# An attention block and a clustering block over four images: places for the first image's stacked keys, and the order of its start

## The chip, the cores and the metric

The kernel runs on one core of one Trainium2 chip. The metric is device time in microseconds (us), the median of three runs. A profile is of one further execution, with its own time. Engines are named as in the profile: PE (matrix products), PEld (loading of their weights, beside PE), ACT (scalar engine), DVE (vector engine), POOL (GpSimd), SP (the queue that issues most DMAs). POOL and ACT issue DMAs too, in the order of their other instructions.

## The reference

Input are four images of 256 channels and 64 x 64 places, in 32-bit floats. The first layer is self-attention over the N = 4096 places of an image, with keys and queries of 32 channels; the second a block of clustering, a two-layer MLP and a pointwise convolution. The change touches the first layer alone, and of it the first image:

```python
xf = x.reshape(B, Cc, N)
q = jnp.einsum('oc,bcn->bno', wq, xf) + bq
k = jnp.einsum('oc,bcn->bon', wk, xf) + bk[None, :, None]
attn = jax.nn.softmax(jnp.einsum('bnd,bdm->bnm', q, k), axis=-1)
v = jnp.einsum('oc,bcn->bon', wv, xf) + bv[None, :, None]
out = jnp.einsum('bcn,bmn->bcm', v, attn).reshape(B, Cc, H, W)
return gamma[0] * out + x
```

The second layer's parts that appear below are wf (a weight that the kernel turns over at the start, with a bias from the table pv_s), wpw (the pointwise weights, from which POOL makes two blocks) and a few tables of constants.

## The kernel before

The 4096 places of an image are cut into eight blocks of 512 (NB). One block of queries against one block of keys is a *unit*; eight units (GRP) make a block of queries, 64 an image. A unit's scores are made in two halves of 128 x 1024 (`half`, `products`, L471); ACT copies each half from PSUM into the unit's slot (`kept`, L484), DVE takes the running maximum `top` from PSUM (L495). The two PSUM tiles for this (pool ps_s) are a ring: a half must wait until the DVE maximum of the half two before it is done. Later, the *weighting* subtracts the maximum (`exps`, L637), takes exponentials on ACT, forms sums of quarter blocks (`factors`, L660 on DVE, L646 on POOL) and multiplies with the values in seven products for eight (`weigh`, L716, tile av). For these products POOL makes four sums and differences of the value blocks of each group of four (`sums`, L646, called by `added`).

Keys and queries are kept as high and low halves, stacked on 128 partitions: of one block of 512 places, 32 channels times four parts. A projection of four blocks (`projected`, L344) gives PSUM tiles from which ACT makes the high half (L361) and DVE the low one (L362). `straight` (L376) stacks one block by four DMAs of 64 KB from these halves into a tile of 128 x 512; `written` (L372) stores the halves in DRAM by four DMAs of 256 KB, from where later units load their stacked blocks by one DMA (`k_unit`, L449; `q_block`, L443). Stacked keys have two places (tag "k"), so keys u + 2 are not loaded before the scores of unit u are done. For the first image, `staged` projects blocks 0 to 3 of k and q into a tile `st`, and `halved` blocks 4 to 7, each into a tile with the tag "t13".

Values are made in pairs of 128 places (`v_pair`, four matmul instructions, eight passes on PE; L426), in one of two PSUM buffers of the pool ps_m, and copied by ACT (L434). 16 pairs make an image; POOL's group g needs pairs 2g and 2g + 1.

Everything is recorded under a manual schedule: each engine does its instructions in the order in which the functions call them. `alone` (L847) is the order of the first image until its weighting begins; later images do this work in the gaps of the image before. In it:

- `roots` (L218 to L294) does square roots for the constants on DVE and ACT, and loads ACT's table;
- three value pairs, `staged`, three more pairs, the sums of groups 0 to 2 on POOL;
- units 0 to 7. After unit 0, k's second projection; after unit 1, q's; after units 2 to 7 one value pair each (6 to 11), and at the odd ones from 3 a group of sums. `k_straight` stacks keys u + 2 at the end of unit u. `written` stores k0, q0, k1, q1 at the ends of units 1 to 4, on POOL's queue. From u = 3, `load_rest` issues a step of the remaining constants on SP: the weights mix, then fvb and wproj, then gbv, pv_s and a table, and last pool_w and wpw_s with POOL's two instructions on wpw (L187, L188). At u = 5 the second block of queries is loaded, at u = 6 `wf` (L282, L285) turns its weights over;
- `fold`, pair 12, the transposes of the maximum (`turned_over`, tile tt, L557), a half of unit 8, pair 13, sums 6, the maximum as a diagonal (`across`, L564 and L566), its spreading over the partitions by PE (`spread`, tile hold, L627), pair 14, `exps(0)`, `factors(0)`, pair 15, the second half of unit 8, sums 7.

The pool `work` has single tiles with the tags "t4", "rden", "acc" and "t", which only the weighting uses: t4 and acc are first written in `factors(0)`, rden and t after the first block of queries.

Of the kernel before, what the change touches and what calls it, by code (L numbers as in the profile page):

```python
# [9 lines left out]
F32R = mybir.dt.float32r  # L10
# [4 lines left out]
P = 128  # L15
# [3 lines left out]
NB = 512  # L19
# [10 lines left out]
RG, GRP = 4, N // NB  # L30
# [30 lines left out]
def attention_then_cluster_block(  # L61
# [17 lines left out]
    nc = tc.nc  # L79
# [3 lines left out]
    big = ctx.enter_context(tc.tile_pool(name="big", bufs=1))  # L83
# [4 lines left out]
    work = ctx.enter_context(tc.tile_pool(name="work", bufs=2))  # L88
# [242 lines left out]
    def attention(b, xs, ys):  # L331
# [5 lines left out]
        qs, ks, slots, mxs, accs, tops, rdens, ts = {}, {}, {}, {}, {}, {}, {}, {}  # L337

        def projected(which, i, ps):

            col = 1 if which == "k" else 0
            for k in range(KC):
                for r in range(RG):
                    nc.tensor.matmul(  # L344
                        ps[r * D : (r + 1) * D],
                        wqk_s[:, k, col],
                        block(xs, k, 4 * i + r),
                        start=(k == 0),
                        stop=(k == KC - 1),
                    )  # L350

        def halves_of(which, hi, lo, ps):

            col = 1 if which == "k" else 0
            if which not in own:
                own[which] = dram.tile([NBLK // RG, P, 4, NB], F32, tag=which, name=f"{which}_{b}")
            bias = bqk_s[:, col : col + 1]  # L360
            nc.scalar.activation(hi, ps, AF.Identity, bias=bias)  # L361
            nc.vector.scalar_tensor_tensor(  # L362
                lo, ps, bias, hi.bitcast(F32), ALU.add, ALU.subtract
            )

        def part_of(which, c, hi, lo):
            return (hi if c in ((0, 2) if which == "k" else (0, 1)) else lo).bitcast(F32)

        def written(which, i, hi, lo, dma=nc.sync):
            rows = own[which][i]  # L370
            for c in range(4):
                dma.dma_start(out=rows[:, c], in_=part_of(which, c, hi, lo))  # L372

        def straight(which, r, dst, hi, lo, other=nc.sync):
            for c in range(4):
                (other if c % 2 else nc.sync).dma_start(  # L376
                    out=dst[c::4].bitcast(F32),
                    in_=part_of(which, c, hi, lo)[r * D : (r + 1) * D],
                )
# [6 lines left out]
        def staged():  # L386

            st = spool.tile([P, 4, NB], F32R, tag="s", name=f"st_{b}")  # L390
            ps = ps_s.tile([P, 2, NB], F32, tag="s", name=f"pr_{b}")
            k0, q0 = (st[:, 0], st[:, 1]), (st[:, 2], st[:, 3])
            for j, w in enumerate("kq"):
                projected(w, 0, ps[:, j])
            halves_of("k", *k0, ps[:, 0])
            k_straight(0, k0)
            qs[0] = work.tile([P, NB], F32R, tag="q", name=f"q_{b}_0")
            halves_of("q", *q0, ps[:, 1])
            straight("q", 0, qs[0], *q0, nc.scalar)
            k_straight(1, k0)  # L400
            return k0, q0

        def k_straight(u, src):
            ks[u] = big.tile([P, NB], F32R, tag="k", bufs=2, name=f"k_{b}_{u}")
            straight("k", u % RG, ks[u], *src)

        def halved(which, i, write=True):

            ps = ps_m.tile([P, NB], F32, tag="m", name=f"{which}p_{b}_{i}")
            two = work.tile([P, 2, NB], F32R, tag="t13", name=f"hl_{which}_{b}_{i}")  # L410
            projected(which, i, ps)
            halves_of(which, two[:, 0], two[:, 1], ps)
            if write:
                written(which, i, two[:, 0], two[:, 1])
            return two[:, 0], two[:, 1]
# [3 lines left out]
        def v_half(i):  # L419
            if i == 0:  # L420
                own["v"] = big.tile([P, N // P, C], F32, tag="v", name=f"v_{b}")
            if i % 2 == 0:
                vps[0] = ps_m.tile([P, 2, C], F32, tag="m", name=f"vp_{b}_{i // 2}")
            o = (i * P) % XT
            for k in range(KC):
                nc.tensor.matmul(  # L426
                    vps[0][:, i % 2, :],
                    xs[i * P // XT][:, k, o : o + P],
                    wv_s[:, k, :],
                    start=(k == 0),  # L430
                    stop=(k == KC - 1),
                )
            if i % 2:
                nc.scalar.copy(own["v"][:, i - 1 : i + 1, :], vps[0])  # L434

        def v_pair(i):
            v_half(2 * i)
            v_half(2 * i + 1)
# [44 lines left out]
        def kept(u, h, sc):  # L483
            nc.scalar.copy(slots[u][:, PAIR[h]].rearrange("p h r n -> p r h n"), tiles(sc))  # L484
# [3 lines left out]
        def highest_of(nb, src):  # L488


            top = tiles(tops[nb])
            if nb not in saved:
                saved[nb] = src
                return
            nc.vector.tensor_tensor(top, src, top if saved[nb] is None else saved[nb], ALU.max)  # L495
            saved[nb] = None
# [6 lines left out]
        def half(u, h, kept_only=False):  # L503

            nb, g = divmod(u, GRP)
            if h == 0:
                begun(u)
            sc = products(u, h)  # L510
            kept(u, h, sc)
            own_copy = slots[u][:, PAIR[h]].rearrange("p h r n -> p r h n")
            if g == 0 and h == 0:
                highest_of(nb, own_copy)
            elif kept_only:
                held.append(lambda: highest_of(nb, own_copy))
            else:
                return lambda: highest_of(nb, tiles(sc))
            return lambda: None
# [40 lines left out]
        def across(nb, tag="w2", tp=None):  # L560
            if tp is None:
                tp = turned_over(nb, ps_m.tile([P, 4, P], F32, tag="m", name=f"tt_{b}_{nb}"))
            mx = small.tile([P, 4], F32, tag="mx", name=f"mx_{b}_{nb}")
            nc.vector.tensor_reduce(mx, tp, AX.X, ALU.max)  # L564
            dg = work.tile([P, 4, P], F32, tag=tag, bufs=1, name=f"dg_{b}_{nb}")
            nc.vector.tensor_tensor(  # L566
                dg,
                ident.unsqueeze(1).to_broadcast([P, 4, P]),
                mx.unsqueeze(2).to_broadcast([P, 4, P]),
                ALU.mult,  # L570
            )
            return dg
# [272 lines left out]
        dgs, t31, t4s = {}, {}, {}  # L845

        def alone():  # L847

            roots()
            for i in range(3):  # L850
                v_pair(i)
            k0, q0 = staged()
            for i in range(3, 6):
                v_pair(i)

            def added(*gs):
                for g in gs:
                    for f in sums(g):
                        f()

            added(0, 1, 2)
            rest = load_rest()
            for u in range(GRP):
                half(u, 0)()
                if u < GRP - 1:
                    half(u, 1)()
                else:

                    sc = products(u, 1)
                    highest_of(0, tiles(sc))  # L870
                    kept(u, 1, sc)
                if u == 0:
                    k1 = halved("k", 1, False)
                elif u == 1:
                    q1 = halved("q", 1, False)
                else:
                    v_pair(u + 4)
                    if u % 2:
                        added((u + 3) // 2)
                if u < 6:  # L880
                    k_straight(u + 2, k0 if u < 2 else k1)
                if 0 < u < 5:
                    written("kqkq"[u - 1], (u - 1) // 2, *(k0, q0, k1, q1)[u - 1], nc.gpsimd)
                if u > 2:
                    next(rest, None)
                if u == 5:
                    q_block(1)
                elif u == 6:
                    wf()
            fold(0)  # L890
            v_pair(12)
            tp = turned_over(0, ps_m.tile([P, 4, P], F32, tag="m", name=f"tt_{b}_0"))
            half(GRP, 0)
            v_pair(13)
            added(6)
            dgs["dg"] = across(0, "w2", tp)
            spread(0, dgs["dg"])
            v_pair(14)
            exps(0)
            factors(0)  # L900
            v_pair(15)
            half(GRP, 1, True)
            added(7)
# [1205 lines left out]
```

## Time and profile before

| | us |
|---|---|
| median of three runs | 3135.86 (3134.9 to 3136.3) |
| the profiled execution, its own time | 3135.99 |
| its span, first to last instruction | 3134.2 |
| PE's first value pair starts | 5.86 |
| first half-score of unit 0 | 25.29 |
| first weighting matmul (L716) | 71.46 |

In the span of 97.0 us from the start, PE is busy for 78.6, DVE for 48.6, ACT for 47.9, POOL for 57.4. The DMAs of the start, as the profile lists them (queue, operation, count, size of each, median us from issue to landing, over the first 150 us):

```profile
k<-st SPq DMA_DIRECT2D x16, 64.0 KB, 2.1
k<-st POOLq DMA_DIRECT2D x4, 256.0 KB, 3.6
q<-st POOLq DMA_DIRECT2D x4, 256.0 KB, 5.2
k<-hl_k SPq DMA_DIRECT2D x16, 64.0 KB, 2.3
```

A row of the timeline is: start, length, engine, line, operation, what it writes and reads, count, and in brackets the idle time of the engine before it with what ended it. A row of the windows is: the stretch, its length, the busy time of each engine with the number of its instructions, the granted clock of PE as a share of full speed, the busy share of the DMA engines, GB/s. "PEq", "SPq" and the like are the sequencers, which issue and wait.

### The profile page before, as it was taken

To read this page: it belongs to the slowest core of one execution; us is meant where nothing else is said; L and a number is where in the kernel's file an instruction comes from. 1 tells how busy PE (TensorE), PEld (TensorE's weight loads), DVE (VectorE), ACT (ScalarE), POOL (GpSimd) and SP (SyncE) were. 2 spreads that over 40 slices of the span, in tenths; PEclk is the share of its full clock that TensorE was granted. 3 is DMA by queue.
4 is the path that set the end of the run, shared out by engine and by line. 5 is a ranking of instruction groups with operands and counts; after the bars stand their busy time and mean duration, and the time that the engine had idled before them with its cause. 6 is when DMAs were issued, how large, how long until landed. Compare 5 with 4: busy or idle time off the path is not lost.

```text
span 3134.2 us, 41370 instructions
## 1 busy us (share of the span) xinstructions
PE 3053.2 (97%) x14210; PEld 2498.2 (80%) x14210; DVE 2514.4 (80%) x3574; ACT 1778.9 (57%) x2817; POOL 2324.7 (74%) x2232
## 2 busy tenths in 40 slices
PE   7999999999999999999999999999999999998999
PEld 5788887788688888878868888886877888875886
DVE  4999888777798888877779888877768988887675
ACT  4666664544566666454456666645446666655344
POOL 5888887477588888647758888955766988893563
PEclk9999999999999999999999999999999999999999
DMA  5112226200112123510011222431011112160000
GB/s 167 45 61 64 61 61 186 71 17 28 48 47 68 55 61 100 154 58 18 28 51 51 65 63 65 113 125 58 28 41 44 59 57 67 54 153 1 14 21 28
DMA packets 105570, 200.40 MB, mean 64 GB/s; under 512 B 14880, under 2 KB 30864, under 8 KB 103824
## 3 DMA queue, kind: packets, MB, share of 16 engines
q1 hardware_dynamic: 100464, 178.66, 18.2%
q0 software_dynamic: 4256, 18.90, 2.9%
q8 instruction: 113, 1.85, 0.2%
q14 instruction: 97, 0.79, 0.1%
q10 hardware_dynamic: 640, 0.20, 0.0%
HBM read 147.01 MB, written 48.34 MB: 62 GB/s over the span
## 4 chain that ended last, share of the span: by engine, by line
PE 74%; DVE 10%; POOL 8%; issue 3%; ACT 3%; DMA 2%; SPq 1%; ACTq 0%; POOLq 0%; DVEq 0%
PE av L716 35%; PE mo L1721 10%; PE sc L471 7%; PE hq L1804 5%; PE hp L1804 3%; PE hr L1804 3%; PE fv L1293 3%; POOL acc L646 2%; DVE top L495 2%; DVE s L637 2%; POOL t L646 2%; POOL s L646 1%; PE mo L1705 1%; DMA w<-in_w 1%; PE vp L426 1%
## 5 line engine op out<-in xcount | busy, mean ns | idle before, releaser
L484 ACT COPY s<-sc 128x1024 f32<-128x1024 f32 x512 | 515.2, 1012 | 433.8 <-PE sc L471 426.3
L637 DVE TENSOR_TENSOR s<-s,hold 128x1024 f32<-128x1024 f32 x512 | 598.6, 1209 | 6.7 <-ACT hold L620 5.0
L646 POOL TENSOR_TENSOR acc<-acc,t 128x512 f32<-128x512 f32 x408 | 541.4, 1347 | 0.0
L716 PE MATMUL av<-s,sum 128*128 128x256 f32 x2048 | 526.9, 380 | 3.7 <-POOL s L646 3.5
L716 PE MATMUL av<-t,v 128*128 128x256 f32 x2048 | 528.0, 380 | 2.5 <-POOL t L646 2.2
L716 PE MATMUL av<-s,v 128*128 128x256 f32 x2048 | 526.7, 380 | 2.1 <-ACT xn L1672 1.1
L646 POOL TENSOR_TENSOR s<-t,s 128x512 f32<-128x512 f32 x256 | 340.5, 1330 | 224.8 <-DVE t L660 157.5
L660 DVE TENSOR_TENSOR t<-s,hold 128x1024 f32<-128x1024 f32 x256 | 311.8, 1218 | 186.6 <-POOL acc L646 95.5
L495 DVE TENSOR_TENSOR top<-sc,top 128x1024 f32<-128x1024 f32 x350 | 426.8, 1219 | 31.4 <-ACT s L484 28.0
L716 PEld LDWEIGHTS av<-s,v 128*128 128x128 f32 x2048 | 387.6, 190 | 64.9 <-ACT xn L1672 2.3
L716 PEld LDWEIGHTS av<-t,v 128*128 128x128 f32 x2048 | 387.9, 190 | 63.2 <-POOL t L646 8.5
L716 PEld LDWEIGHTS av<-s,sum 128*128 128x128 f32 x2048 | 388.1, 190 | 61.3 <-POOL s L646 8.5
L1759 ACT ACTIVATE hs<-hs,pv_s 128x256 f32<-128x256 f32 x496 | 232.5, 502 | 352.6 <-DVE hs L1795 352.6
L471 PE MATMUL sc<-q,k 128*128 128x512 f32 x1024 | 394.2, 469 | 24.8 <-ACT s L484 9.5
L1721 PE MATMUL mo<-hs,w 128*128 128x256 f32 x1512 | 384.8, 381 | 0.0
L646 POOL TENSOR_TENSOR t<-s 128x512 f32<-128x512 f32 x256 | 330.7, 1292 | 46.8 <-PE av L716 33.4
L1721 PEld LDWEIGHTS mo<-hs,w 128*128 128x128 f32 x1512 | 283.8, 190 | 46.8 <-ACT hs L1759 6.2
L641 ACT ACTIVATE hold<-s 128x512 f32<-128x512 f32 x256 | 154.2, 602 | 212.5 <-DVE s L637 210.7
L1795 DVE TENSOR_TENSOR hs<-hq,hs 128x256 f32<-128x256 f32 x496 | 198.7, 421 | 85.9 <-PE hq L1804 75.9
L643 ACT ACTIVATE s<-s 128x1024 f32<-128x1024 f32 x256 | 266.9, 1043 | 0.0
L471 PEld LDWEIGHTS sc<-q,k 128*128 128x128 f32 x1024 | 175.5, 191 | 113.7 <-DVE top L495 54.2
L716 PE MATMUL av<-t,sum 128*128 128x256 f32 x1024 | 262.4, 378 | 0.0
(296 smaller groups left out, 4871.3 us busy)
## 6 DMA issues: line engine op xcount, KB each, us to landing
k<-k SPq DMA_DIRECT2D x248, 256.0 KB, 2.7
x<-in_x SPq DMA_DIRECT2D x62, 512.0 KB, 6.8
out<-xn SPq DMA_DIRECT2D x62, 256.0 KB, 2.1
att<-t SPq DMA_DIRECT2D x56, 256.0 KB, 4.0
x<-att POOLq DMA_DIRECT2D x12, 1024.0 KB, 10.0
w<-in_w SPq DMA_DIRECT2D x8, 1024.0 KB, 12.0
q<-q SPq DMA_DIRECT2D x31, 256.0 KB, 4.0
rden<-row_rd SPq DMA_DIRECT2D x28, 256.0 KB, 3.6
```

The lines of the kernel that those rows point to most:

```text
L471: nc.tensor.matmul(sc[:, r, :], k_s[:, (2 * h + r) * P : (2 * h + r + 1) * P], qs[u // GRP], start=True, stop=True,)
L484: nc.scalar.copy(slots[u][:, PAIR[h]].rearrange("p h r n -> p r h n"), tiles(sc))
L495: nc.vector.tensor_tensor(top, src, top if saved[nb] is None else saved[nb], ALU.max)
L637: nc.vector.tensor_tensor(sh, sh, mb.to_broadcast([P, 2, 2, QW]), ALU.subtract)
L643: nc.scalar.activation(s[:, PAIR[1]], s[:, PAIR[1]], AF.Exp)
L646: nc.gpsimd.tensor_tensor(out, x, y, op)
L660: nc.vector.tensor_tensor(t31[u], s[:, B11 : B22 + 1 : 2], b12.to_broadcast([P, 2, 2, QW]), ALU.add)
L716: nc.tensor.matmul(av[bank][:, half_ * QW : (half_ + 1) * QW], a[:, r], t[:, r], start=(g == 0 and r == 0 and i in (1, 7, 2, 4)), stop=(g ...
L1721: return nc.tensor.matmul(bank[:, half * HB : (half + 1) * HB], a[:, j], t, start=start, stop=stop)
L1759: nc.scalar.activation(src, src, AF.Gelu_apprx_tanh, bias=pvc("b1", P, j + 4 * (i > 1)))
L1795: nc.vector.tensor_tensor(dst, ps, term, ALU.add)
L1804: nc.tensor.matmul(out, w, x, start=True, stop=True)
```

## The change

Eight stacked blocks of keys get eight places: keys 0 and 1 the two of the tag "k", keys 2 and 3 the tiles "t4" and "rden", keys 4 and 5 the halves of "acc", 6 and 7 those of "t". `staged` stacks keys 1 to 3 at once, and keys 4 to 7 are stacked one after the other after k's second projection. The first projection comes after two value pairs instead of three, so that from there every pair comes one place later in the order: pairs 5 to 10 in units 2 to 7, 11 before the transposes, 12 and 13 between them and hold. Sums are called at even units (2, 3, 4 at u = 2, 4, 6), group 5 after pair 11. `written` goes to units 2 to 5; the steps of constants begin at u = 1. On POOL, the two instructions on wpw stand, after it, before the writes of q1 and the sums of group 4. On SP, the order is now keys 0, query 0, keys 1 to 7, then all constants, the second block of queries and keys 8.

```diff
@@ staged
-            k_straight(1, k0)
+            for u in range(1, 4):
+                k_straight(u, k0)
             return k0, q0
 
         def k_straight(u, src):
-            ks[u] = big.tile([P, NB], F32R, tag="k", bufs=2, name=f"k_{b}_{u}")
+            if u < 2:
+                ks[u] = big.tile([P, NB], F32R, tag="k", bufs=2, name=f"k_{b}_{u}")
+            elif u < 4:
+                tag = ("t4", "rden")[u - 2]
+                ks[u] = work.tile([P, NB], F32R, tag=tag, bufs=1, name=f"k_{b}_{u}")
+            elif u % 2 == 0:
+                tag = ("acc", "t")[u // 2 - 2]
+                two = work.tile([P, 2, NB], F32R, tag=tag, bufs=1, name=f"k_{b}_{u}")
+                ks[u], ks[u + 1] = two[:, 0], two[:, 1]
             straight("k", u % RG, ks[u], *src)
@@ alone
-            for i in range(3):
+            for i in range(2):
                 v_pair(i)
             k0, q0 = staged()
-            for i in range(3, 6):
+            for i in range(2, 5):
                 v_pair(i)
...
-            added(0, 1, 2)
+            added(0, 1)
...
                 if u == 0:
                     k1 = halved("k", 1, False)
+                    for i in range(4, GRP):
+                        k_straight(i, k1)
                 elif u == 1:
                     q1 = halved("q", 1, False)
                 else:
-                    v_pair(u + 4)
-                    if u % 2:
-                        added((u + 3) // 2)
-                if u < 6:
-                    k_straight(u + 2, k0 if u < 2 else k1)
-                if 0 < u < 5:
-                    written("kqkq"[u - 1], (u - 1) // 2, *(k0, q0, k1, q1)[u - 1], nc.gpsimd)
-                if u > 2:
+                    v_pair(u + 3)
+                    if u % 2 == 0:
+                        added(u // 2 + 1)
+                if 1 < u < 6:
+                    written("kqkq"[u - 2], (u - 2) // 2, *(k0, q0, k1, q1)[u - 2], nc.gpsimd)
+                if u:
                     next(rest, None)
...
             fold(0)
-            v_pair(12)
+            v_pair(11)
+            added(5)
             tp = turned_over(0, ps_m.tile([P, 4, P], F32, tag="m", name=f"tt_{b}_0"))
             half(GRP, 0)
+            v_pair(12)
+            dgs["dg"] = across(0, "w2", tp)
             v_pair(13)
             added(6)
-            dgs["dg"] = across(0, "w2", tp)
             spread(0, dgs["dg"])
```

## The prediction, made before the changed kernel ran

> **What bounds the kernel now.** I read the page's busy shares first, then the chain of waits for 0 to 200 us, the timeline of the matmul engine and the windows of the first 97 us, and last the DMA landings there. The page:
>
> ```profile
> PE 3053.2 (97%) x14210; PEld 2498.2 (80%) x14210; DVE 2514.4 (80%) x3574; ACT 1778.9 (57%) x2817; POOL 2324.7 (74%) x2232
> ```
>
> PE is the bound nearly everywhere, and the engines run their instructions in program order, so what the first image's start saves on PE moves all that follows. Only that start is changed. Its PE timeline (start, length, instruction, in brackets the idle time before and what ended it):
>
> ```profile
> 13.17 1.99 PE L426 MATMUL vp<-wv_s,x 128*128 128x256 f32 x8 [1.11 <-ACT v L434]
> 15.09 3.64 PE L344 MATMUL pr<-x,wqk_s 128*32 128x512 f32 x32
> ...
> 38.37 2.05 PE L471 MATMUL sc<-q,k 128*128 128x512 f32 x4 [3.25 <-DMA k<-st]
> ...
> 56.66 0.74 PE L285 MATMUL wf_p<-ident,pv_s 96*128 96x96 f32 x2 [3.89 <-DMA pv_s<-in_pv]
> 57.11 2.05 PE L471 MATMUL sc<-q,k 128*128 128x512 f32 x4
> ...
> 63.99 0.60 PE L557 MATMUL tt<-ident,top 128*128 128x128 f32 x4
> ...
> 66.66 1.04 PE L627 MATMUL hold<-dg,ones 128*128 128x512 f32 x2
> ```
>
> Three holes: 1.11 us before the third value pair, 3.25 us before unit 3's scores (its stacked keys are not there), 3.89 us before the bias part of wf (pv_s is not there). The windows (span, busy us of PE, PEld, DVE, ACT, POOL, then the granted clock):
>
> ```profile
> 38.40:57.10 18.70, 14.22 (x52) 10.39 (x53) 9.80 (x8) 10.06 (x12) 9.34 (x15) 0.87 0.62 194
> 57.10:71.50 14.40, 14.40 (x57) 11.49 (x57) 7.47 (x7) 7.11 (x12) 7.20 (x10) 0.83 0.28 74
> ```
>
> A mean of 0.87 over 18.7 us and 0.83 over 14.4 us is, if the clock is either full or half, 4.9 us at half clock in each. The first weighting matmul (av) starts at 71.46. I call this moment the end of the front, and forecast its move.
>
> **The change part by part.**
>
> (a) Projection behind two pairs. The third pair waits for a PSUM buffer that ACT frees at 13.1, after its start-up work. Now pr comes straight after pair 1, whose last matmul is issued at 11.68 and leaves PE at about 11.9; its last x half, issued at 3.99, landed 7.3 us later, at 11.3. So pr goes from 15.09 to 11.9: **3.2 us**. Three value pairs follow it in either kernel, ACT's copies of pairs 0 and 1 (until 13.6) are over before it needs the projection at 15.6, and the q and k DMAs begin at 16.3 instead of 19.5, as the x loads end (the last lands at 16.4). All of units 0 to 2 moves by 3.2 us.
>
> (b) Keys 2 and 3 in places of their own. Before, keys 3 wait on SP for unit 1's scores, are issued from 30.02, and go among POOL's writes of k and q (issued from 28.50). Landing times of keys 3, then of keys 1, which had the queues to themselves:
>
> ```profile
> DMA to landing us min/median/max: 3.2/5.2/5.9
> ...
> DMA to landing us min/median/max: 2.1/2.1/2.1
> ```
>
> Now keys 1, 2, 3 follow each other on SP at the 0.635 us per issue that keys 1 show: 20.2, 22.7, 25.2 to 27.8, landed by 29.9. Unit 3 needs them after unit 2's scores and its pair, at 31.8. So the hole goes: unit 3 starts at 31.8 instead of 38.37, **6.6 us** in sum.
> A rule speaks against this. The Trainium skill, "DMA: Bandwidth & Descriptors", section "Issuing engines are not separate DMA queues": DMAs of SP, ACT and POOL share the same 16 DMA engines and interleave. By it, moving POOL's writes or SP's keys only moves the collision; if keys 2 to 7 took the 5.2 us median instead of 2.1, keys 3 would land at 33 and (b) would lose 1.2 us. The row agrees on the sharing, but POOL's first write now stands behind value pair 5 (copied at 32.5) and four sums (3.2 us): 35.8, 6 us after keys 3 have landed. I take 2.1. The collision comes with keys 7 and the constants (d).
>
> (c) Units 3 to 6. Without waits a unit is held by the ring score (0.73), ACT copy (1.01), DVE maximum (1.23), with the value copy (0.59) in ACT's way: stepping through these durations puts the second half-scores of units 3 to 6 at 33.0, 36.2, 39.6 and 42.8 and the pair of unit 6 at 43.2 to 45.0. wf comes at 45.0 instead of 52.4: 13.2 us for four units where the trace has 14.0, part of that at half clock. **+0.8, sum 7.4.** Keys 4 to 7 are 16 DMAs on SP behind keys 3: 27.8 to 37.9, the last landed at 42.3 even at +5. Unit 4 (35.2) and unit 7 (45) find them.
>
> (d) The constants. They begin one step earlier relative to keys (from u = 1), but stand behind all 16 issues. pv_s is the seventh of them. SP issues from 37.9, while POOL's 2 MB of writes are under way (35.8 to about 46). In the same situation before (writes of k1 and q1 issued from 45.87) pv_s was issued 8.4 us and landed 10.75 us after the writes began; there 0.47 MB of SP's DMAs stood before it (five of 64 KB, 48, 96 and little ones), here 0.8 (keys 7 with 256 KB, twice 192 for the mix weights, 48, 96). So 10 to 12 us after 35.8: 45.8 to 48. I take 47.0, nearer the row. Against 45.4, where the transposes of wf end, a wait of 1.6 remains of 3.89: **+2.3, sum 9.7.** Ends: no wait (+3.9) and the whole wait (0). Two other users of these writes have room: the slot of unit 7 needs the staging tile free at 48 (q's last write lands at about 46), and q_1 and k_8 land by 50 to 51, needed at 53.
>
> (e) Unit 7 to the transposes of the maximum: 56.66 to 63.99 is 7.3 us, mostly at half clock. At full clock the chain is wf and ACT's two copies of it (1.35), ACT's score copy (1.0), two maxima (2.45), the fold (0.8) and some 0.05 to 0.1 at each of three handovers: 5.8 us: **+1.5, sum 11.2.**
>
> (f) Order at the end. Before, one pair lies between the transposes and hold (2.67 us, and DVE's diagonal is ready at 66.52, just in time). Now pairs 12 and 13 do: 0.35 + 0.45 + 2 x 1.73 + 0.2 = 4.5. PE works in it, but hold starts DVE's and ACT's exponentials, behind which av waits; two pairs cover them as before (4.8 us from hold to av). **-1.85, sum 9.35.**
>
> (g) Half clock that stays. The skill, "TensorE: Matmul & The Clock Gate", section "What's actually happening", says that the clock is halved after an idle window of about 3.4 us and that windows are free-running. By it the 1.6 us of (d) cost nothing. The rows of this trace:
>
> ```profile
> 235.00:245.00 10.00, 7.96 (x30) 6.30 (x29) 8.36 (x10) 3.89 (x7) 6.52 (x6) 0.83 0.30 89
> 598.00:612.00 14.00, 9.86 (x40) 6.44 (x41) 11.75 (x26) 10.88 (x16) 9.96 (x8) 1.00 0.13 39
> 1369.00:1385.00 16.00, 13.89 (x42) 10.08 (x41) 11.25 (x26) 10.62 (x15) 9.95 (x8) 0.68 0.12 33
> ```
>
> A gap of 2.04 us at 238 and one of 1.33 at 1371 were followed by half clock, one of 1.33 at 601 was not. So the rule's length is not safe here; a window of 3.4 us costs up to 1.7. I take **-0.5**, sum **8.85**; ends 0 and -1.7.
>
> (h) POOL. The wait for wpw_s now stands before the writes of q1 and three groups of sums. Before:
>
> ```profile
> 60.44 0.45 POOL L187 TENSOR_TENSOR wpw_s<-wpw_s 128x128 f32<-128x128 f32 x1 [7.11 <-DMA wpw_s<-in_wpw]
> ...
> 73.61 1.28 POOL L646 TENSOR_TENSOR s<-t,s 128x512 f32<-128x512 f32 x1 [3.68 <-DVE t L660]
> ```
>
> Now wpw_s lands at about 50, behind it come 1.0 + 2.15 (four issues) + 3 x 3.2 = 12.8 us, so POOL is free at 62.8. Its first product of the weighting is wanted at 73.6 - 8.8 = 64.8. Cost nothing, with 2 us of cover: from a landing at 52 each us costs one.
>
> From 62 on the order on every engine is as before, so the move stays. The profiled execution took 3135.99 (span 3134.2), 0.13 over the median 3135.86. 3135.99 - 8.85 = 3127.1; I say **3127.2 us**.
>
> **The rivals.**
> 1. The constants wait on: SP issues at the 0.75 to 1.87 us that its keys 7 show before, pv_s lands at 49.5 or later, and 3.89 us stay (2.3 less), with a half-clock window (1 less): gain 5.5, 3130.5. For it: those issues. Against: SP starts the constants only 2 us after the writes begin.
> 2. pv_s comes in time: gain 9.35 + 1.6 = 10.95, 3125.0. For it: they follow each other without key waits. Against: 2 MB on the same DMA engines.
> 3. POOL takes over: wpw_s lands at 54.5 instead of 50, its 2.5 us beyond the cover are lost: 3129.7. For it: POOL's 7.11 us wait. Against: SP now issues it some 10 us earlier.
> 4. Slower: the same POOL queue, far later. Its 12.8 us behind the wait eat the whole gain when wpw_s lands at 60.9, about where it lands now (60.4); then every us is lost. At 68 it is 7 us: 3143. For it: nothing in SP's queue but crowding; it would need 16 key issues at over 1.5 us each.
> 5. The keys wait in spite of their places: the program's waits show no PE wait on keys 2 to 7 any more; I give it nothing of its own.
>
> **How the numbers follow.** Forecast 0.60, rival 1 0.17, rival 2 0.10, rival 3 0.08, rival 4 0.05. The range holds (d) and (g) at their ends and rivals 1 to 3: 3124.3 to 3131.5; the rest outside is rival 4 and the tails. Later half-clock windows fall anew (the one at 1371 costs 2 us: that image's step from gap to gap is 772.3 against 770.3 for the one before), which is within it. 0.2% is 6.3 us, about what a measurement tells from no change: faster means below 3129.6. Faster: nearly all of the forecast and rival 2, half of rivals 1 and 3, 0.78. Same 0.17, slower 0.05.
>
> **What would show it.** pr at 11.9; no idle time before unit 3, which starts near 31.8; the wait before wf's bias 0 to 2.5 us and ended by pv_s; mean clock over 0.95 from 30 to 62; tt to hold 4.5 us; av at 62.6; POOL idle before its first product. Wrong it would be if unit 3 still waited for keys, if POOL had no idle time there, or if av moved and a later stage gave it back.

## The result, and the profile after

| | before | changed |
|---|---|---|
| median (17 runs each), us | 3134.32 | 3129.48 |
| profiled execution, us | 3135.99 | 3129.87 |
| its span, us | 3134.2 | 3128.1 |
| first projection `pr` starts, us | 15.09 | 12.41 |
| first weighting matmul `av` starts, us | 71.46 | 67.35 |

The ratio is 0.9985, 95% interval [0.9979, 0.9992]: a gain of 4.8 us (2.5 to 6.6), where 8.85 was worked out. In the profiled execution 4.11 of the 6.12 us are won by the first weighting matmul. The other 2 us come later, most of them in one place: DVE's instructions are 4.63 us ahead of those of before at 2822 and 6.33 us ahead at 2836. Between, before ran at half clock for 3.41 us from 2830.3, and the changed kernel did not. That the change removed this stretch is not shown: e2 (below), whose front is 11 us faster than that of before, has it too, from 2822.3. (A longer stretch of before, 10.24 us from 1372.9, put the changed kernel 1.8 us further ahead for a time; by 1735 the lead was back at 4.7.)

PE's timeline of the changed kernel, the rows that answer to those of before (L482, L285, L568, L638 and L727 are L471, L285, L557, L627 and L716 of before):

```profile
12.41 3.64 PE L344 MATMUL pr<-x,wqk_s 128*32 128x512 f32 x32
...
32.14 0.73 PE L482 MATMUL sc<-q,k 128*128 128x512 f32 x2
...
46.39 0.40 PE L282 MATMUL wf_p<-ident,mix_first 128*96 128x128 f32 x2 [0.74 <-ACT v L445]
50.99 0.74 PE L285 MATMUL wf_p<-ident,pv_s 96*128 96x96 f32 x2 [4.20 <-DMA pv_s<-in_pv]
...
58.17 0.60 PE L568 MATMUL tt<-ident,top 128*128 128x128 f32 x4
...
62.57 1.02 PE L638 MATMUL hold<-dg,ones 128*128 128x512 f32 x2
...
67.35 2.01 PE L727 MATMUL av<-s,v 128*128 128x256 f32 x8
```

Two of the three holes are gone: none before the third value pair, none before unit 3 (32.14, no bracket). The third is longer than it was, 4.20 us against 3.89. Unit 3 came 6.2 us earlier, and behind the hole only 5.7 of that were left (50.99 against 56.66). Windows of the changed kernel, and then of before for the ten microseconds from 40 (stretch, length, busy time of PE, PEld, DVE, ACT, POOL, granted clock, DMA share, GB/s):

```profile
38.40:57.10 18.70, 12.97 (x47) 9.71 (x47) 9.59 (x9) 7.82 (x11) 10.08 (x18) 0.82 0.90 282
57.10:71.50 14.40, 14.14 (x64) 11.26 (x63) 7.38 (x7) 7.55 (x12) 10.79 (x14) 1.00 0.18 57
40.00:50.00 10.00, 5.76 (x24) 4.17 (x24) 4.95 (x5) 4.57 (x6) 4.83 (x8) 0.97 0.95 311
```

```profile
40.00:50.00 10.00, 9.41 (x35) 6.57 (x34) 7.31 (x6) 7.07 (x9) 6.26 (x11) 0.92 0.53 156
```

The column before the last tells the story. From 40 to 50 us the DMA engines of the changed kernel are busy for 0.95 of the time and PE for 5.76 of 10 us; before, it was 0.53 and 9.41. Keys 4 to 7, the constants and k1's writes, all earlier by the change, and the writes of k0 and q0, which it moved later (issued from 35.44, from 28.50 before), now share those ten microseconds. A clock of 0.82 in the first row is 6.83 us at half clock, which begin at 49.34, in the hole: as long a stretch as the one from 55.31 before. An earlier one of before, 3.41 us from 38.24 behind the hole for keys 3, is gone.

POOL in the changed kernel, its wait for wpw_s and its first product of the weighting:

```profile
53.32 0.45 POOL L187 TENSOR_TENSOR wpw_s<-wpw_s 128x128 f32<-128x128 f32 x1 [8.26 <-DMA wpw_s<-in_wpw]
...
69.50 1.28 POOL L657 TENSOR_TENSOR s<-t,s 128x512 f32<-128x512 f32 x1 [2.83 <-DVE t L671]
```

POOL waits long, and still stands idle for 2.83 us before its first product.

### The profile page after: what moved, and what is told of

It is laid out like the page before. It is cut to its first block, busy times and chain, and to the rows that moved or that the text cites. A ratio compares the mean times of both kernels' runs of the same rounds, so it can differ in the third digit from the quotient of the medians.

```text
span 3128.1 us, 41373 instructions
## 1 busy us (share of the span) xinstructions
PE 3046.1 (97%) x14210; PEld 2492.9 (80%) x14210; DVE 2514.0 (80%) x3574; ACT 1779.9 (57%) x2817; POOL 2327.1 (74%) x2232
## 4 chain that ended last, share of the span: by engine, by line
PE 72%; DVE 11%; POOL 8%; issue 3%; ACT 3%; DMA 2%; SPq 1%; POOLq 0%; ACTq 0%; DVEq 0%
PE av L727 34%; PE mo L1734 10%; PE sc L482 7%; PE hq L1817 5%; PE hp L1817 3%; PE hr L1817 3%; PE fv L1306 3%; POOL acc L657 3%; DVE top L506 2%; POOL t L657 2%; DVE s L648 2%; POOL s L657 1%; PE mo L1718 1%; DMA w<-in_w 1%; PE hq_pw L1817 1%
## 5 line engine op out<-in xcount | busy, mean ns | idle before, releaser
L727 PE MATMUL av<-s,sum 128*128 128x256 f32 x2048 | 526.9, 380 | 3.7 <-POOL s L657 3.5
L727 PE MATMUL av<-t,v 128*128 128x256 f32 x2048 | 527.2, 380 | 2.5 <-POOL t L657 2.2
L727 PE MATMUL av<-s,v 128*128 128x256 f32 x2048 | 525.9, 379 | 2.5 <-ACT t L757 1.3
L727 PEld LDWEIGHTS av<-s,v 128*128 128x128 f32 x2048 | 387.2, 189 | 65.3 <-ACT xn L1685 2.3
L727 PEld LDWEIGHTS av<-t,v 128*128 128x128 f32 x2048 | 387.5, 190 | 63.2 <-POOL t L657 8.5
L727 PEld LDWEIGHTS av<-s,sum 128*128 128x128 f32 x2048 | 387.9, 190 | 61.2 <-POOL s L657 8.8
L482 PE MATMUL sc<-q,k 128*128 128x512 f32 x1024 | 393.1, 468 | 24.2 <-ACT s L495 10.5
L482 PEld LDWEIGHTS sc<-q,k 128*128 128x128 f32 x1024 | 174.3, 189 | 112.5 <-DVE top L506 56.9
L727 PE MATMUL av<-t,sum 128*128 128x256 f32 x1024 | 262.4, 378 | 0.0
```

The costliest lines, as they stand in the source:

```text
L482: nc.tensor.matmul(sc[:, r, :], k_s[:, (2 * h + r) * P : (2 * h + r + 1) * P], qs[u // GRP], start=True, stop=True,)
L727: nc.tensor.matmul(av[bank][:, half_ * QW : (half_ + 1) * QW], a[:, r], t[:, r], start=(g == 0 and r == 0 and i in (1, 7, 2, 4)), stop=(g ...
```

## The experiments

My theory after the result: pv_s is late because the DMA engines are full between 36 and 51 us, so the order in which transfers are given to them decides. Rivals: the half clock behind the hole, the place of hold, or POOL, whose wait for wpw_s now comes earlier. In the table, "pr to av" takes out where PE started, since `pr` began anywhere from 10.99 to 12.57 us in the twelve profiles that have it behind two pairs. The medians are of 5 to 17 runs on several chips; each ratio is to before on the same chip, with its interval.

| run | pr | av | pr to av | median us | ratio |
|---|---|---|---|---|---|
| before | 15.09 | 71.46 | 56.4 | 3134.32 | 1 |
| e14_places_alone | 15.71 | 72.19 | 56.5 | 3134.39 | 0.9996 [0.9987, 1.0005] |
| e4_only_two_pairs | 11.82 | 69.92 | 58.1 | 3133.57 | 0.9997 [0.9988, 1.0006] |
| e10_no_poolwait_alone | 12.24 | 70.06 | 57.8 | 3132.2 | 0.9992 [0.9984, 1.0001] |
| e3_writes_back | 12.57 | 70.21 | 57.6 | 3130.91 | 0.9989 [0.998, 0.9998] |
| changed kernel | 12.41 | 67.35 | 54.9 | 3129.48 | 0.9985 [0.9979, 0.9992] |
| e7_hold_first | 12.15 | 67.10 | 55.0 | 3129.36 | 0.9983 [0.9975, 0.9992] |
| e9_pv_mix_hold | 11.14 | 66.48 | 55.3 | 3130.18 | 0.9985 [0.9976, 0.9993] |
| e8_pv_mix_no_poolwait | 12.25 | 66.11 | 53.9 | 3130.26 | 0.9986 [0.9977, 0.9995] |
| e2_pv_mix_early | 11.86 | 60.45 (+5.56) | 48.6 (+5.56) | 3128.64 | 0.9979 [0.9971, 0.9988] |
| e12_late_second_halves_alone | 11.24 | 64.22 | 53.0 | 3128.41 | 0.998 [0.9971, 0.9989] |
| e1_pv_early | 10.99 | 63.88 | 52.9 | 3127.28 | 0.9977 [0.9968, 0.9985] |
| e13_pv_early_late_second_halves | 11.18 | 60.38 | 49.2 | 3125.1 | 0.9969 [0.9957, 0.9981] |
| e11_late_second_halves | 12.25 | 61.05 | 48.8 | 3124.82 | 0.9968 [0.9955, 0.998] |

**The constants given earlier.** e1 issues pv_s right behind the x loads, before the keys; e2 the two mix weights as well.

```diff
-    pv_s = loaded("pv_s", pv, [P, NPV])
+    pv_s = const.tile([P, NPV], F32, name="pv_s")
+    nc.sync.dma_start(out=pv_s, in_=pv)
@@ load_rest, since pv_s has left the list of tables that it steps through
-            if i == 2:
+            if i == 1:
@@ alone (e2 only)
+            rest = load_rest()
+            next(rest)
             roots()
...
             added(0, 1)
-            rest = load_rest()
```

> The changed kernel with pv_s alone (7 KB) issued on SP right behind the x loads. Theory 'crowd' (half of the forecast gain is lost because pv_s stands behind 16 key DMAs and constants among POOL's writes): no wait for pv_s, wf opens at 46.4 when the mix weights land and its bias part follows at 46.8 instead of 50.99; the clock stays full from 49 to 57; the first weighting matmul comes at 63 to 64.5 instead of 67.35; time 3 to 4 us under the changed kernel (about 3126). Rival 'next wait' (wpw_s on POOL, query 1 and keys 8, or the slot of unit 7 are just as late): the first weighting matmul stays above 66 and the time within 1 us of the changed kernel.

The wait is gone, and av comes at 63.88, within what was expected. The median is 3127.28, 2.2 us under the changed kernel where 3 to 4 were expected, and the intervals of the two ratios overlap. Short waits are left: 1.29 us for the mix weights, 1.43 for ACT's copy of the value pair before tt, 1.02 for the keys of unit 8. The clock did not stay full as expected: it was half for 3.41 us from 53.18.

> pv_s and the mix weights (384 KB) behind the x loads. Theory 'crowd': as with pv_s alone, wf about 0.8 us sooner (45.6) and all later constants 2.5 us sooner, so that POOL's wait for wpw_s ends near 51; first weighting matmul at 62 to 63.5, 4 to 5 us under the changed kernel. Rival: 384 KB at the start delay keys 0 and query 0 (unit 0 at 23.5 or later instead of 22.55) and take back 1 us or more.

The front did more than was expected, av at 60.45 and not 62 to 63.5, and unit 0 at 21.70 was not held up. But the median is only 0.8 us under the changed kernel. e2 also moves each later step of the constants one unit forward, and with them POOL's two instructions on wpw_s, ahead of the sums of group 3 and of k1's writes. PE's next row with a hole, and POOL's wait, in e2:

```profile
71.60 2.08 PE L728 MATMUL av<-s,sum 128*128 128x256 f32 x4 [5.56 <-POOL s L658]
```

```profile
49.86 0.85 POOL L188 TENSOR_TENSOR wpw_s<-wpw_s 128x128 f32<-128x128 f32 x1 [10.97 <-DMA wpw_s<-in_wpw]
```

Four sums' groups and eight DMA issues stood behind that wait; POOL's first product came at 70.28, and 5.56 us of the gain went back. This is the mechanism of the forecast's rival 3, in another kernel.

**Parts of the change.** e3 puts the writes back to units 1 to 4. e4 is the kernel before with the two pairs and the order of pairs that goes with them. e14 is the kernel before with the eight places alone.

```diff
@@ e3
-                if 1 < u < 6:
-                    written("kqkq"[u - 2], (u - 2) // 2, *(k0, q0, k1, q1)[u - 2], nc.gpsimd)
+                if 0 < u < 5:
+                    written("kqkq"[u - 1], (u - 1) // 2, *(k0, q0, k1, q1)[u - 1], nc.gpsimd)
@@ e14, against before: k_straight as changed, and
-            k_straight(1, k0)
+            for u in range(1, 4):
+                k_straight(u, k0)
...
                     k1 = halved("k", 1, False)
+                    for i in range(4, GRP):
+                        k_straight(i, k1)
...
-                if u < 6:
-                    k_straight(u + 2, k0 if u < 2 else k1)
```

> The changed kernel with the writes of halves at the ends of units 1 to 4, as before the change. Theory 'crowd': POOL's first 2 MB are out of the way by about 34, pv_s lands at 43 to 46 instead of 50.95, the wait before wf's bias falls from 4.2 to under 1 us; keys 2 and 3 land up to 3 us later, for which unit 3 waits 0 to 1.5 us; first weighting matmul at 63.5 to 65. Rival (the one unit's delay was needed): unit 3 waits for its keys until 36 or later, as before, and the first weighting matmul comes at 67 or later.

Missed. Units 4 and 5 found their keys, but unit 2 waited 1.25 us for its own, and q0, k1 and q1 came together from 36.5 to 46, as POOL's sums stood between; the mix weights landed at 51.5 and were waited for 4.47 us, pv_s another 1.52.

> The kernel before with the two value pairs ahead of the projection alone (and the order of pairs, sums and hold that goes with it); places of keys, writes and constants as before. By the sum: 2.7 us from the projection, 1.8 lost again between the transposes and hold, so first weighting matmul at 70 to 71 and 0 to 1.5 us under the kernel before. Rival (the later keys and constants follow the projection only in part): first weighting matmul at 71.5 or later, no gain.

As expected, to within 0.1 us: pr comes 3.27 us earlier and av 1.54. Waits for keys 2 (1.95 us) and keys 6 (3.98 us) take the rest, while the one for pv_s is gone.

> The kernel before with the eight places alone: keys 1 to 3 stacked at once, keys 4 to 7 behind k's second projection; the first projection, the value pairs, the writes and the steps of constants stay where they were. It tells what the places are worth without the rest of the change. My theory: the hole of 3.25 us before unit 3 goes (unit 3 at 35.1 in place of 38.37); keys 3 and 4 run beside POOL's first writes from 28.5 and are stretched but in time; the constants come 2 to 3 us earlier than before and still collide with k1's and q1's writes, so the wait before the bias of wf stays at 3 to 5 us; the first weighted sum comes at 68 to 69 us (71.46 before), the time 2 to 3.5 us under before. Rival: as in e3_writes_back, with the writes in their old places the crowd is worse and the constants land no earlier than before; then the first weighted sum stays at 70.5 or later and the time within 1 us of before.

The rival is right, and it corrects how I had read step (b). Unit 3 in e14:

```profile
38.78 2.05 PE L480 MATMUL sc<-q,k 128*128 128x512 f32 x4 [2.55 <-DMA k<-st]
```

Keys 3 had their place and were issued from 29.96, but POOL's writes ran from 29.11, and the last piece landed 6.1 us after its issue, at 38.69. A place removes the wait on SP, not the transfers beside it. Alone, neither the places nor the pairs move the time measurably. With both and the early constants, but the old writes (e3), the ratio is 0.9989 and pr to av 57.6 us; with the writes one unit later as well, 0.9985 and 54.9. The fronts are apart, the intervals of the two ratios are not. Later writes without the places were not tried.

**The place of hold.** e7 puts `spread(0)` ahead of pair 13.

```diff
             dgs["dg"] = across(0, "w2", tp)
+            spread(0, dgs["dg"])
             v_pair(13)
             added(6)
-            spread(0, dgs["dg"])
```

> The changed kernel with hold issued right after the scores across the gap, ahead of the fourteenth value pair. My theory: in the changed kernel the PE's front is one line of work, so the place of hold costs what the forecast's step (f) says: tt to hold falls from 4.40 us by 1.7 to 1.8 us, hold starts near 60.8 and the first weighted sum near 65.5 us (67.35 in the changed kernel), and the kernel takes 1.5 to 2 us less, about 3127.7. Rival: the weighted sum waits for the first product on POOL (69.50 us in the changed kernel, with 2.83 us of slack before it) or for the value pair that is now issued later; then the first weighted sum stays above 66.5 and the time moves less than 0.7 us.

My theory fell. Hold comes 2.05 us earlier (60.52), av only 0.25. PE has no idle time between tt and av, so the pair that no longer stands before hold stands behind it: 9.18 us from tt to av in the changed kernel, 9.25 in e7. The 1.7 us longer way from tt to hold that the change brings is the value pair that it no longer has ahead of tt, not a cost that another place would save.

**POOL's wait.** e10 moves the two instructions on wpw_s from the steps of constants to the end of the derived weights, in the first image's weighting; e8 does this in e2, e9 adds e7's hold.

```diff
-        nc.gpsimd.tensor_tensor(pw_q[1], pw_q[1], pw_q[3], ALU.add)
-        nc.gpsimd.tensor_scalar(pw_q[3], pw_q[3], -1.0, None, ALU.mult)
         yield
@@ the derived weights
+        todo.append(lambda: nc.gpsimd.tensor_tensor(pw_q[1], pw_q[1], pw_q[3], ALU.add))
+        todo.append(lambda: nc.gpsimd.tensor_scalar(pw_q[3], pw_q[3], -1.0, None, ALU.mult))
         return todo
```

> The changed kernel with POOL's two instructions on wpw_s moved to the end of the derived weights and nothing else. It tests whether POOL's wait of 8.26 us for wpw_s bounds the changed kernel. My theory: it does not (POOL had 2.83 us idle before its first product at 69.50); the first weighted sum stays at 67.35 within 1 us, POOL's idle before the first product grows to some 9 to 11 us, and the time stays within 1 us of the changed kernel. Rival: the wait does bound the start of the weighting; then PE's idle after 67 us shrinks and the time falls by 2 us or more.

> The changed kernel with pv_s and the two mix weights behind the x loads, as in e2_pv_mix_early, and POOL's two instructions on wpw_s taken out of the load steps and put at the end of the derived weights, in the first image's weighting. My theory: what e2 gave back (5.56 us of PE idle at 71.60) was POOL's 10.97 us wait for wpw_s ahead of its sums; with that wait gone POOL's first product comes near 62.6 us and not 70.28, the first weighted sum stays near 60.5 and no gap over 1 us follows it; the time is 5 to 6.5 us under the changed kernel, 3123 to 3125. Rival: the sums on POOL are held up by the queue of writes or by VectorE's results and not by wpw_s; then the first product stays above 68 and the gap at 71 remains with 4 us or more, the time near e2's 3128.6.

> e8_pv_mix_no_poolwait with hold right after the scores across the gap. My theory: both gains add, the first weighted sum near 58.7 us, the time 1.5 to 2 us under e8, about 3122. Rival: at that pace the next wait decides (POOL's product near 62.6, the last value pairs, or the softmax behind hold); then the first weighted sum may start near 59 but idle time of 1.5 us or more follows, and the time is within 0.7 us of e8.

All three missed, and for one reason. POOL's wait does not bound the changed kernel: without it (e10) av comes later, at 70.06, and not earlier. The wait had held q1's writes back until 54.4. Without it they start at 44.9, and pv_s, 7 KB, is issued only at 49.04 and lands at 53.22; PE waits 6.39 us for it. In e8 POOL writes k1 and q1 from 42.39 to 46.7, and this is what PE meets:

```profile
55.69 1.18 PE L483 MATMUL sc<-q,k 128*128 128x512 f32 x2 [2.04 <-DMA k<-k]
```

Keys of unit 8 are late, after 1.46 us for keys 7 and 1.31 for ACT, and 3.41 us at half clock follow. Hold first (e9) gained nothing again, its wait for the keys of unit 8 was 3.21 us.

**The second halves' writes later.** What e2's front had and e8's lacked was that k1 and q1 were written after 54 us. They are read from DRAM only for later blocks. e12 moves these eight writes behind the sums of group 5, in the changed kernel; e13 does so in e1, e11 in e8, both without POOL's early wait (e8 has none, in e13 it is taken out too).

```diff
-                if 1 < u < 6:
-                    written("kqkq"[u - 2], (u - 2) // 2, *(k0, q0, k1, q1)[u - 2], nc.gpsimd)
+                if 1 < u < 4:
+                    written("kq"[u - 2], 0, *(k0, q0)[u - 2], nc.gpsimd)
...
             added(5)
+            written("k", 1, *k1, nc.gpsimd)
+            written("q", 1, *q1, nc.gpsimd)
             tp = turned_over(0, ps_m.tile([P, 4, P], F32, tag="m", name=f"tt_{b}_0"))
```

> The changed kernel with the second halves' writes behind the sums of pair 5, nothing else. My theory: k1's writes at 42.9 to 50.2 us are a part of what made pv_s late (landed 50.95); without them it lands near 49, the half clock behind it stays, the first weighted sum comes near 65.5 us, and the time is 1 to 2.5 us under the changed kernel, unless POOL's sums, now some 2 us later, take it back. Rival: pv_s is late by SP's issue behind the keys alone (k0's and q0's writes), then it lands at 50.5 or later and the time does not move by more than 0.7 us.

> e1_pv_early with the second halves' writes behind the sums of pair 5 and POOL's two instructions on wpw_s in the weighting. My theory: the mix weights land earlier than e1's 48.7 us, the wait of 1.29 us before the bias goes, the ninth unit's keys land before 53, and the first weighted sum starts at 61 to 62.5 us (63.88 in e1), the time 1.5 to 3 us under e1's 3127.3. Rival: the value pairs' evictions on ACT and the half clock set the pace from 50 us on; then the first weighted sum stays at 63 or later and the time within 0.8 us of e1.

> e8_pv_mix_no_poolwait with the second halves' writes (k1, q1; 8 DMAs, 4.3 us of POOL) moved from units 4 and 5 to behind the sums of pair 5, where POOL is idle and where e2 had them by way of its wait. My theory: what kept e8 slow were these 2 MB running at 42 to 52 us against the loads (keys 7 landed 46.9, keys of the ninth unit 56.2); with them later, keys of the ninth unit land near 52, the first weighted sum starts near 60.5 us as in e2 and POOL's first product comes before 64.5, so no gap over 1.5 us follows; the time is 4.5 to 6.5 us under the changed kernel, 3123 to 3125. Rival: the writes then collide with what is loaded next or hold POOL's sums up; the product comes after 66 and the time stays within 1.5 us of e1's 3127.3.

In e12 pv_s lands at 48.61; of the 2.3 us against the changed kernel 1.2 are the earlier start of pr. The other 1.2 fit k1's writes, but are no measure of them (see (d) below). Av comes at 64.22, earlier than the 65.5 expected, and 3.4 us at half clock remain; in time the difference from the changed kernel, 1.1 us, is within the intervals. The two mix weights on SP, first in the changed kernel and then in e12 (issue time in ns, min/median/max; first and last start), and e12's window from 40 us:

```profile
L167 SPq DMA_DIRECT2D mix_first<-in_wfv x2: 1418/1500/1583, 41.0 to 42.6; - x2
```

```profile
L167 SPq DMA_DIRECT2D mix_first<-in_wfv x2: 501/543/585, 42.8 to 43.5; - x2
```

```profile
40.00:50.00 10.00, 6.11 (x28) 4.47 (x27) 4.36 (x4) 4.50 (x8) 1.63 (x3) 1.00 0.71 188
```

The DMA share fell from 0.95 to 0.71, and SP issued the mix weights in a third of the time, though it came to them later, at 42.8. e13 and e11 came out as expected, e13's front somewhat earlier; PE and POOL of e13:

```profile
44.75 0.40 PE L283 MATMUL wf_p<-ident,mix_first 128*96 128x128 f32 x2 [0.31 <-DMA mix_first<-in_wfv]
...
60.38 2.01 PE L728 MATMUL av<-s,v 128*128 128x256 f32 x8
```

```profile
54.64 2.15 POOL L373 DMA_DIRECT2D k<-hl_k  x4
56.79 2.13 POOL L373 DMA_DIRECT2D q<-hl_q  x4
```

The hole for pv_s and the half clock of the front are gone, of the waits only 0.31 us for the mix weights and 1.44 for ACT before tt are over 0.3 us between 44 and 60 us. At 3125 us these two are the lowest medians, some 4.5 us under the changed kernel; they were not timed beside it on one chip, and the ends of the intervals still touch (0.998 and 0.9979). Against e8, from which e11 differs in the writes alone, the medians are 5.4 us apart (on two chips; the intervals touch there too, 0.998 and 0.9977) and the fronts 5.1 us.

Over all rows of the table the median follows the front: a straight line through move of av (for e2 with its 5.56 us) and ratio has 0.8 us of time per us of av and misses no row by more than 1.4 us. What follows av (in e2, av with its 5.56 us) takes 3059.4 to 3062.8 us in the fourteen profiled executions, 3060.7 in the changed kernel. The two fastest fronts, e13 and e11, have 3062.1 and 3062.3, before 3062.8. So later stages take back little of what a front wins, and less than single executions scatter.

## Why the prediction was right in sign and nearly twice too large

| step | worked out | measured |
|---|---|---|
| (a) pr | 11.9 | 12.41 |
| (b) pr to unit 3 | 19.9 | 19.73 |
| (c) transposes of wf | 45.0 | 46.39 |
| (d) pv_s, and the wait for it | 47.0, 1.6 | 50.95, 4.20 |
| (e) bias of wf to tt | 5.8 | 7.18 |
| (f) tt to hold | 4.5 | 4.40 |
| av | 62.6 | 67.35 |

Of the 4.75 us by which av came late, 0.5 lie in (a), 3.5 more up to the bias of wf, in (d), and 0.9 behind it, beyond the 0.5 that (g) had set aside. That 3129.48 lies only 2.3 us above the 3127.2 forecast is in part luck: the gain is 4.0 us short, but before itself has a median of 3134.32 in 17 runs and not the 3135.86 of three from which the forecast was counted.

(a) Right in kind, 0.5 us less: the first two pairs ended later than read off the trace of before. In the other eleven profiles pr lies on both sides of 11.9.

(b) The number was right. But the places alone do not give it: in e14, with POOL's writes where they were, 2.55 of the 3.25 us stay. The later start of these writes, which the step named as its condition, is needed. Whether it would do without the places is open.

(c) The transposes of wf came 1.4 us late: 0.5 from (a), and 0.74 is a wait for ACT's value copy. It cost nothing, since pv_s decided.

**(d) is the step that failed.** "10 to 12 us after 35.8" was read from a situation with 2 MB of writes; pv_s landed 15.5 us after the writes began and not 11.2. Two terms were mis-sized. First, "POOL's 2 MB of writes are under way (35.8 to about 46)" leaves out k1's writes, which POOL issued from 42.90 in the middle of the constants: 3 MB. Second, keys 4 to 7 were put on SP at 0.635 us each, until 37.9: the last four were issued in 0.59, 0.81, 1.45 and 1.37 us, one of keys 3 before them in 1.19, and SP is done with the keys at 40.9, 2.5 us later counted from pr.

e12, without k1's writes, and e10, with q1's as well, give three doses. From the start of the writes to the landing of pv_s it takes 14.3 us with 2 MB, 15.5 with 3 and 17.9 with 4; from SP's first issue of constants, 5.8, 10.0 and 11.9. So the writes that were left out count, but e12, with the very 2 MB that the step assumed, is still 3 us over 11.2: there SP was done with the keys only at 42.84, 31.6 us after pr against 28.5 in the changed kernel, though the two kernels are the same up to k1's writes. How the miss divides between the two terms is not shown, only that both are in it.

e1 takes pv_s out of the crowd. From pr to av it needs 52.9 us, the changed kernel 54.9, the forecast 50.7: half of the miss is the wait for pv_s itself. The rest is in the waits that e1 still has and its half clock. e13 and e11, with k1's and q1's writes out of the way as well, need 49.2 and 48.8.

(e) and (g): 6.83 us at half clock followed the hole of 4.20 us, where I had reckoned with full clock and 0.5 us. In e2 and e11, at full clock, the way from bias to tt takes 6.2 us; so 0.4 us were too few instructions counted (ACT's value copy ends last, 1.0 us of wait), and 1.0 was clock. The mean clock from 30 to 62 us was 0.89, where over 0.95 was to be the sign. The rule of the Trainium skill ("TensorE: Matmul & The Clock Gate", section "What's actually happening", half clock after an idle window of about 3.4 us) fits this gap by its length, but half clock began after 2.55 us of it. In e12 half clock began 1.4 us after a gap of 2.54, and in e1 1.1 us after a gap of 1.43, in the middle of one of 1.02, while e13's 1.44 and e11's 1.00 were followed by none before 220 us. As in before, the length of a gap does not decide; the last section shows what these traces do follow.

(f) The size was right; e7 shows that it is work and not a wait.

(h) POOL's cover held. wpw_s landed at 53.25 and not at 50, but the front came later too. Rival 3 was not this kernel's case; e2 shows its price where the front is faster, 5.56 us.

Of the rivals it was the first, the constants that wait on, 3130.5 worked out and 3129.48 measured. What was said to speak against it, that SP starts the constants only 2 us after the writes begin, was wrong by that second term: it started them 5.5 us after (40.95 against 35.44).

## What to carry to other kernels

When a change lets transfers start earlier, list everything that will be in flight in the stretch where they land, every queue's, with bytes, before a landing time is taken from a quieter row. Here it paid to give a small table that somebody waits for ahead of the bulk (e1), and to put bulk writes that nobody reads soon behind the loads that decide (e11 against e8). A wait that looks idle can be what keeps a queue's later transfers out of the way: e10 took one away and its front came 2.7 us later, e8 took it away and lost in the front the 5.6 us that it won behind it.

## What was not expected of the hardware

- SP's issue of a DMA was long where landing was slow: the same 64 KB of keys took 0.59 us to issue and 2.1 to land on quiet queues, and 1.45 and 6.35 among POOL's writes (DMA share 0.95 from 40 to 50 us). In e14 the 7 KB of pv_s landed 7.58 us after its issue. The issue time is the worse part, since it delays everything behind it on SP. Whether SP waits for the DMA engines or for its own earlier transfers is not shown; one issue of keys 3 took 1.19 us at 25.77 in the changed kernel, 10 us before POOL's first write, when the two DMAs before it took 3.2 and 2.7 us to land.
- In the twelve profiles with two pairs ahead of it, the first projection began between 10.99 and 12.57 us. A front is to be compared from its own start, and even then SP's issue of the same keys scattered by 3 us between two executions (e12 and the changed kernel); differences below 1 us between two single profiles say little.
- In these traces the clock follows how busy PE was in windows, not the length of one gap. In each of the fourteen profiles the half-clock stretches between 17 and 3060 us are 3.41, 6.83, 10.24 or 13.65 us long and lie on one grid of 3.41 us. Of the windows of this grid at full clock, all 39 with PE busy for under 0.43 of the time were followed by half clock, 24 of 110 between 0.43 and 0.64, and none of 12208 above. Rows (the first number behind the comma is PE's busy time): the changed kernel's window in the hole (0.40 of 3.41 us) and the one after it, e12's with 2.01 of its gap of 2.54, e1's with the gap of 1.43 and the start of the next, and the two over which e13's gap of 1.44 falls, which no half clock followed:

```profile
45.93:49.34 3.41, 0.40 (x2) 0.17 (x2) 0.75 (x1) 0.35 (x1) 0.00 (x0) 1.00 0.90 309
49.34:52.76 3.42, 1.77 (x5) 1.58 (x6) 0.00 (x0) 0.59 (x3) 0.00 (x0) 0.50 0.95 181
46.64:50.05 3.41, 1.40 (x7) 1.23 (x8) 0.00 (x0) 0.79 (x3) 0.00 (x0) 1.00 0.65 107
49.77:53.18 3.41, 1.50 (x8) 0.81 (x7) 1.82 (x3) 1.99 (x3) 1.46 (x3) 1.00 0.87 285
46.93:50.34 3.41, 2.82 (x14) 2.14 (x12) 3.14 (x3) 0.79 (x2) 0.63 (x1) 1.00 0.99 248
50.34:53.76 3.42, 2.57 (x14) 2.30 (x15) 1.38 (x2) 2.30 (x4) 2.39 (x3) 1.00 0.26 93
```

The same kind of window tells apart two gaps that the forecast could not. In before, the gap of 1.33 us at 1371, which half clock followed, lies in a window with PE busy for 0.53, the one at 601, which none followed, in one with 0.61. What decides between 0.43 and 0.64 stays open.
